# Regrouping the token tiles of the first mixture-of-experts pass, with a new hand-written plan of units

## The chip, the core and the metric

The kernel runs on one core of a Trainium2 chip. The metric is the device time of one execution in microseconds; each version's figure is the median of several runs. Engines are named as in the profile: PE is TensorE's matmuls, PEld its weight loads, DVE is VectorE, ACT ScalarE, POOL GpSimd, and SP the engine that issues most of the DMAs ("SPq", "POOLq" are queues).

## The reference

The input is `x`, 8 sequences of 512 tokens of 128 features, in 32-bit floats. A block of three parts is computed:

```python
x = x + 0.5 * ffn(layernorm(x))     # mixture of experts
x = x + attention(layernorm(x))     # 16 heads of 8, causal, partly rotary
x = x + 0.5 * ffn(layernorm(x))     # the same experts and weights again
```

In `ffn` a router (128 by 8) gives each token 8 logits. The two largest choose two experts, and their softmax gives two weights. An expert is `relu(x @ W1 + b1) @ W2 + b2`, 128 to 512 to 128 features; a token's result is the weighted sum of its two experts.

## The kernel before

**Tokens and passes.** A sequence is four tiles of 128 tokens. The feed-forward doesn't multiply every token with every expert. Tokens are normalised and routed by sequence, and each token's row is scattered twice, by indirect DMA from POOL, into a table in device memory (`xs`) that has room for `cap` rows per expert. Then the experts work through their rows. This is done in six passes, or groups: f0, f1, f2 for the first feed-forward, g0, g1, g2 for the second. Each group has its tiles of tokens and its room per expert (`ROOMS`: tiles, room, whether tagged). Before, f0 holds sequences 0 and 1 (8 tiles, room 351), f1 holds 2 to 4 and f2 holds 5 to 7 (12 tiles each, room 480); g0 holds 6 tiles (room 256), g1 and g2 hold 13 each (room 512). If an expert got more rows than its room, a flag would start a second, general path behind the main one.

**One expert of one group** (`experts`) is a list of pieces. SP fetches the expert's rows (`fetch`, L957; it waits for every scatter of the group). `turn` transposes the tiles on PE (L1000) and copies them out. Four `wide` pieces each multiply 128 of the 512 hidden features with all rows of the group's room (L1013) and apply bias and relu (L1020 on ACT, L1022 on DVE). One `out` piece per tile of rows multiplies back (L1037), adds the bias on DVE (L1041), and the last stores the expert's results by SP (L1048) into `ys`. A group of `ct` tiles of rows has 8 x (1 + 4 + `ct`) + 1 pieces: 65 for f0, 73 for f1, f2, g1 and g2, 57 for g0. `combine` then gathers each token's two results by indirect DMA (POOL) and adds them into `x`; in g1 and g2 POOL sends the results home instead (`send`, L981), and `collect` adds them.

**Routing** (`route`) is a stream of steps for one sequence: normalise in three steps (`layernorm`: statistics; aggregates on DVE and `rstd` on POOL; the scaling at L774 on DVE), transpose on PE (L789), logits (L825), ranks, places in the table (L869 and on), then the entry of eight scatters in a queue of jobs, then the gates. `project` does the same for attention's operands in eight steps: layernorm in three, transpose (L789), two for qkv (L1169), rotary, and the write of the operands' tiles.

**Attention** runs over 96 units, 12 to a sequence: 4 groups of 4 heads, 3 units each. A unit computes scores (L1231), their exp on ACT (L1238), a causal minimum with a mask on DVE (L1245), and the product with the values of the unit before (L1257). The score tile has one buffer.

**The order is written out by hand.** PE, ACT, DVE and SP execute in the order in which the program emits instructions, and the emission goes unit by unit, from -30 to 125 (0 to 95 hold attention). `plan` says for each group in which unit its first rows are fetched, and between which units its pieces are emitted. `surround(n)` emits unit n: scores, the values of the unit before, one piece of expert work, one transfer (a scatter or a gather from the queue of jobs), the streams that are `due` in this unit with some pieces between them, the rest of the unit's quota of pieces, and a second transfer where something urgent waits. `at(u, stream, steps, each)` puts `each` steps of a stream into each unit from u on. The quota is the rest of the group's pieces over the rest of its units, rounded up.

**What holds POOL back.** Every transfer waits for a "mark", the last relu, bias add or mask that was emitted before it (`behind_mark`), so that transfers don't bunch up ahead of the work. Before the first relu is emitted there is no mark. POOL's operations keep the program's order.

**Loading.** At the start SP loads the inputs and four experts' weights and clears the tables; the other weights, sequences and clears are issued two a unit from unit -30 on.

Of the kernel before, what the change touches and what calls it, by code (L numbers as in the profile page):

```python
# [21 lines left out]
B, N, D = 8, 512, 128  # L22
# [26 lines left out]
ROOMS = [(8, 351, False), (12, 480, False), (12, 480, False), (13, 512, True), (13, 512, True)]  # L49
# [1284 lines left out]
def macaron_kernel(  # L1334
# [51 lines left out]
    with ExitStack() as main:  # L1386
# [6 lines left out]
        f0 = m.open_group(whole(0, 1), 351, 0, "f0")  # L1393
        f1 = m.open_group(whole(2, 3, 4), 480, 1, "f1")
        f2 = m.open_group(whole(5, 6, 7), 480, 2, "f2")
# [40 lines left out]
        def routed(u, shares, urgent=False, ahead=False):  # L1436
# [6 lines left out]
            if shares[0][0] is not f1:  # L1443
                at(u, r, 3)
                u += 3
            at(u, r, steps)

        def combined(u, g, i, dst=None, urgent=False, ahead=False):
# [4 lines left out]
            (f0, first, first, -16), (f1, -17, -16, 7), (f2, 5, 7, 43), (g0, 41, 43, 79),  # L1453
            (g1, 78, 79, tail - 1), (g2, tail - 2, tail - 1, ends),
# [3 lines left out]
        def surround(n, att):  # L1458

            m.unit = n  # L1460
            now = None
            for g, fetch, start, end in plan:
# [5 lines left out]
                if start <= n < end:  # L1468
                    now, until = fills[g.key], end
                    if g is g1 and att:  # L1470
                        until = end + 7
            quota = min(now[1], -(-now[1] // (until - n))) if now else 0
# [30 lines left out]
            if n >= core and len(m.jobs) + len(m.results) > 2:  # L1503
# [8 lines left out]
        with m.banks(("m", 8)):  # L1512

            n = [m.normalise(b) for b in range(5)]
            r = [m.route([(f0, 0)], early=True), m.route([(f0, 1)], early=True),
                 m.route([(f1, 0)], True, early=True)]
# [3 lines left out]
            step(r[1], r[1], r[1], n[2], n[2])  # L1520
            transfers(8)
            step(n[3], n[3], n[4], n[4], *[r[0], r[1]] * 3, n[2], n[2])
            step(r[2], r[2], r[2], n[3], n[4], n[3], n[4])
            run(*r[:2], *n)
            m.bias_columns()

            at(first, r[2], 4)
            routed(first + 1, [(f1, 1)], urgent=True)
            routed(first + 3, [(f1, 2)], urgent=True)
            routed(-22, [(f2, 0)], urgent=True)  # L1530
            combined(-16, f0, 0, urgent=True, ahead=True)
            routed(-14, [(f2, 1)], urgent=True)
            combined(-12, f0, 1, urgent=True)
            routed(-10, [(f2, 2)], urgent=True)
            at(-10, m.project(0), 8)
            for b in range(B):
                u = b * seq
                if b == 2:
# [3 lines left out]
                if b > 0:  # L1542
                    at(u - 10, m.project(b), 8)
# [85 lines left out]
```

## Time and profile before

| | |
|---|---|
| median of 11 runs | 696.17 us (694.7 to 698.31) |
| profiled execution | 693.42 us, of which the span from first to last instruction is 691.7 |
| PE busy | 620.7 us, 90% of the span |
| DVE, ACT, POOL busy | 405.9, 342.9, 295.4 us |
| scores of unit 0 begin | 143.14 us |
| first transposes of g2 | 607.66 us |
| last matmuls of g2 begin | 665.72 us |

The profile is one execution. In a timeline a line gives the start, the duration of the (merged) instructions, engine, line of the kernel, operation, output and inputs, shape and count; in brackets stands how long the engine was idle before it and what released it. Matmuls are pipelined, so a single matmul's duration is longer than its distance to the next. In a row of slices each digit is the busy tenth of one fortieth of the span.

### The profile page before, as it was taken

The numbers are of one execution on the slowest core, as the hardware profiler recorded it, in microseconds if no ns is written. First come the engines' busy times: TensorE is split into PE (matmuls) and PEld (weight loads), VectorE is DVE, ScalarE is ACT, GpSimd is POOL, SyncE is SP. The second block draws the span as 40 slices with busy tenths as digits, with TensorE's granted clock in tenths as the row PEclk, the third lists the DMA queues.
The fourth block names the chain that finished last, engine by engine and source line by source line (L and its number), as shares of the span: only waits on it lengthen the run. The fifth ranks groups of instructions, "written<-read, shape, count | busy, mean of one in ns | idle before, by whom it ended". The sixth has DMA issues, their size and how long they took to land. (4 is left out here: it accounts for less than half of the span.)

```text
span 691.7 us, 12906 instructions
## 1 busy us (share of the span) xinstructions
PE 620.7 (90%) x4797; PEld 402.0 (58%) x4797; DVE 405.9 (59%) x1432; ACT 342.9 (50%) x552; POOL 295.4 (43%) x318
## 2 busy tenths in 40 slices
PE   3269999999999999999999999989999998989970
PEld 2148867766556556555656656555556566757760
DVE  6736438735466675675676687777666654333424
ACT  4034443454755665466466566566646542244420
POOL 3744637643122314325044324333244556665560
PEclk9999999999999999999999999999999999999995
DMA  8746843312409951001211101112202111154314
GB/s 266 197 136 196 223 115 100 85 49 78 100 20 159 209 169 38 27 24 46 68 32 44 52 26 37 31 32 77 56 28 63 32 58 39 47 152 137 90 55 153
DMA packets 80229, 61.32 MB, mean 89 GB/s; under 512 B 7400, under 2 KB 73888, under 8 KB 80160
## 3 DMA queue, kind: packets, MB, share of 16 engines
q1 hardware_dynamic: 71296, 42.79, 24.3%
q0 software_dynamic: 8576, 17.63, 8.5%
q8 instruction: 40, 0.66, 0.4%
q14 instruction: 29, 0.24, 0.1%
q10 hardware_dynamic: 288, 0.01, 0.0%
HBM read 26.21 MB, written 34.19 MB: 87 GB/s over the span
## 5 line engine op out<-in xcount | busy, mean ns | idle before, releaser
L1238 ACT ACTIVATE ee<-st 128x768 f32<-128x768 f32 (+1 forms) x192 | 159.0, 881 | 90.6 <-PE st L1231 86.7
L479 POOL DMA_INDIRECT yt_f<-ys,back_f x64 | 65.1, 1018 | 128.8 <-DVE ee L1245 55.9
L1245 DVE TENSOR_TENSOR ee<-ee,keep 128x256 f32<-128x256 f32 (+1 forms) x192 | 93.3, 507 | 22.1 <-ACT ee L1238 22.0
L1037 PEld LDWEIGHTS y_f<-w_sb,h_f 128*120 128x120 f32 (+1 forms) x704 | 85.9, 183 | 28.4 <-issue 16.2
L1231 PE MATMUL st<-qT,kT 32*128 32x512 f32 (+3 forms) x1024 | 96.1, 467 | 5.7 <-ACT kT L1214 3.3
L895 POOL DMA_INDIRECT xs<-xn_g,to_g x64 | 63.8, 997 | 84.5 <-DVE ee L1245 32.5
L1037 PEld LDWEIGHTS y_g<-w_sb,h_g 128*128 128x128 f32 x640 | 81.0, 192 | 32.2 <-issue 25.4
L1037 PE MATMUL y_f<-w_sb,h_f 128*120 128x128 f32 (+1 forms) x704 | 93.9, 277 | 0.2 <-DVE h_f L1022 0.2
L1013 PE MATMUL z_g<-xT_g,w_sb 128*128 128x512 f32 (+1 forms) x192 | 89.8, 554 | 1.3 <-DVE e_g L933 0.7
L1257 PE MATMUL o<-ee,vpad 128*32 128x512 f32 (+3 forms) x1024 | 89.6, 442 | 0.8 <-DVE ee L1245 0.8
L1013 PE MATMUL z_f<-xT_f,w_sb 128*128 128x480 f32 (+1 forms) x192 | 89.3, 554 | 1.0 <-ACT xT_f L1004 1.0
L1020 ACT ACTIVATE h_f<-z_f,b1T 128x480 f32<-128x480 f32 (+1 forms) x86 | 53.4, 622 | 68.7 <-PE z_f L1013 67.9
L1037 PE MATMUL y_g<-w_sb,h_g 128*128 128x128 f32 x640 | 85.6, 279 | 0.5 <-DVE o_tok L1280 0.3
L981 POOL DMA_INDIRECT ys<-ysb_g,home_g x64 | 62.8, 981 | 50.4 <-ACT h_g L1020 15.9
L1020 ACT ACTIVATE h_g<-z_g,b1T 128x512 f32<-128x512 f32 (+1 forms) x77 | 49.3, 642 | 54.3 <-PE z_g L1013 54.0
L1041 DVE TENSOR_TENSOR ysb_f<-y_f,b_sb 120x128 f32<-120x128 f32 (+1 forms) x88 | 25.1, 288 | 77.7 <-PE y_f L1037 74.0
L1041 DVE TENSOR_TENSOR ysb_g<-y_g,b_sb 128x128 f32<-128x128 f32 x80 | 23.1, 290 | 76.7 <-PE y_g L1037 72.8
L1231 PEld LDWEIGHTS st<-qT,kT 32*128 32x128 f32 x1024 | 43.1, 183 | 39.0 <-ACT kT L1214 11.4
L1257 PEld LDWEIGHTS o<-ee,vpad 128*32 128x32 f32 x1024 | 23.7, 108 | 52.4 <-issue 5.5
L895 POOL DMA_INDIRECT xs<-xn_n,to_f x40 | 39.0, 974 | 35.3 <-ACT xi_sb L732 8.4
L1013 PEld LDWEIGHTS z_g<-xT_g,w_sb 128*128 128x128 f32 x192 | 29.9, 194 | 21.2 <-issue 12.2
L1013 PEld LDWEIGHTS z_f<-xT_f,w_sb 128*128 128x128 f32 x192 | 30.5, 195 | 14.0 <-issue 7.4
(185 smaller groups left out, 768.3 us busy)
## 6 DMA issues: line engine op xcount, KB each, us to landing
xs<-zeros SPq DMA_DIRECT2D x8, 520.0 KB
xb_g<-xs SPq DMA_DIRECT2D x16, 260.0 KB
w_sb<-in_L_ffn_W_dram SPq DMA_DIRECT2D x16, 256.0 KB
xb_f<-xs SPq DMA_DIRECT2D x16, 240.0 KB
ys<-ysb_f SPq DMA_DIRECT2D x16, 240.0 KB
ys<-zeros SPq DMA_DIRECT2D x2, 1664.0 KB
x<-in_L_attn_x_dram SPq DMA_DIRECT2D x8, 256.0 KB
xs<-zeros SPq DMA_DIRECT2D x1, 1920.0 KB
```

The lines of the kernel that those rows point to most:

```text
L479: ins = op(*args, **kw)
L895: ins = nc.gpsimd.indirect_dma_start(out=g.xs[:, :], out_offset=bass.IndirectOffsetOnAxis(ap=to[:, t, r : r + 1], axis=0), in_=xn[:, t, : ...
L981: ins = nc.gpsimd.indirect_dma_start(out=g.ys[:, :], out_offset=bass.IndirectOffsetOnAxis(ap=home[e][:rows, t : t + 1], axis=0), in_=ys[:r ...
L1013: nc.tensor.matmul(z[:, :n], self.w1_sb[:, e, ts(c, P)], xT[:, n0 : n0 + n], start=True, stop=True,)
L1020: ins = nc.scalar.activation(dst, z[:, :n], AF.Relu, bias=bias)
L1037: nc.tensor.matmul(y[:rows], h[:, c, ts(t, rows)], self.w2_sb[:, e, c, :], start=(c == 0), stop=(c == C - 1),)
L1041: ins = nc.vector.tensor_tensor(ys[:rows, t, :], y[:rows], self.b2_sb[:rows, e], ALU.add)
L1231: nc.tensor.matmul(st[:, h, c0 : c0 + N - kt * P], kT[r0 : r0 + SLOT, ts(kt, P)], qT[r0 : r0 + SLOT, kt * P :], start=True, stop=True,)
L1238: nc.scalar.activation(ee[:, two, :width], st[:, two, :width], AF.Exp)
L1245: ins = self.nc.vector.tensor_tensor(d, d, self.keep.unsqueeze(1).unsqueeze(1).to_broadcast([P, 2, len(parts), P]), ALU.min,)
L1257: self.nc.tensor.matmul(self.o[h * SLOT : (h + 1) * SLOT, kt * P :], self.vpads[b % 2][:, kt, 4 * g + h, :], ee[:, h, c0 : c0 + n], start= ...
```

## The change

The first feed-forward takes the division that the second has: f0 gets sequence 0 and half of 1 (6 tiles, room 256), f1 the rest of 1, all of 2 and 3 and three tiles of 4 (13 tiles, room 512), f2 the last tile of 4 and 5 to 7 (13 tiles, room 512). So sequences 1 and 4 are routed into two groups at once, and combined from two. The pieces become 57 for f0 and stay at 73 for f1 and f2.

The plan moves with it: f0 takes 10 units instead of 14, f1 the units -20 to 0 instead of -16 to 6, f2 1 to 36 instead of 7 to 42, g0 38 to 73 instead of 43 to 78, and g1 starts at 74 instead of 79. Unit 37 has no expert work. In g0 and g1 the quota is spread evenly over attention's units instead of being rounded up in each. At the start f0's dispatch has 12 scatters instead of 16, the normalisations of sequences 2 to 4 are taken ahead of the last four of them, and units before -20 may take a third transfer. The projections of sequences 1 and 4 and their second routings take two steps a unit (`each`), the projections from 6 and 7 units ahead of the sequence's attention instead of 10.

```diff
-ROOMS = [(8, 351, False), (12, 480, False), (12, 480, False), (13, 512, True), (13, 512, True)]
+ROOMS = [(6, 256, False), (13, 512, False), (13, 512, False), (13, 512, True), (13, 512, True)]
...
-        f0 = m.open_group(whole(0, 1), 351, 0, "f0")
-        f1 = m.open_group(whole(2, 3, 4), 480, 1, "f1")
-        f2 = m.open_group(whole(5, 6, 7), 480, 2, "f2")
+        f0 = m.open_group([(0, 0, T), (1, 0, 2)], 256, 0, "f0")
+        f1 = m.open_group([(1, 2, T), *whole(2, 3), (4, 0, 3)], 512, 1, "f1")
+        f2 = m.open_group([(4, 3, T), *whole(5, 6, 7)], 512, 2, "f2")
...
-        def routed(u, shares, urgent=False, ahead=False):
+        def routed(u, shares, urgent=False, ahead=False, each=1):
             early = u < 0 or u > core
             r = m.route(shares, urgent, ahead, early)
             steps = 7 if early else 8
             if u > core:
                 at(u, r, 3 + steps, 3)
                 return
-            if shares[0][0] is not f1:
-                at(u, r, 3)
-                u += 3
-            at(u, r, steps)
+            at(u, r, 3 + steps, each)
...
         plan = [
-            (f0, first, first, -16), (f1, -17, -16, 7), (f2, 5, 7, 43), (g0, 41, 43, 79),
-            (g1, 78, 79, tail - 1), (g2, tail - 2, tail - 1, ends),
+            (f0, first, first, -20), (f1, -21, -20, 1), (f2, 0, 1, 37), (g0, 37, 38, 74),
+            (g1, 73, 74, tail - 1), (g2, tail - 2, tail - 1, ends),
         ]
...
                     now, until = fills[g.key], end
-                    if g is g1 and att:
-                        until = end + 7
-            quota = min(now[1], -(-now[1] // (until - n))) if now else 0
+                    quota = min(now[1], -(-now[1] // (until - n)))
+                    if g in (g0, g1) and att:
+                        until = end + 7 * (g is g1)
+                        quota = g.pieces - now[1]
+                        quota = g.pieces * (n + 1 - start) // (until - start) - quota
...
-            if n >= core and len(m.jobs) + len(m.results) > 2:
+            if (n >= core or n < -20) and len(m.jobs) + len(m.results) > 2:
                 run(take(fill, todo // 2))
                 todo -= todo // 2
                 m.transfer(second=True)
...
-            r = [m.route([(f0, 0)], early=True), m.route([(f0, 1)], early=True),
-                 m.route([(f1, 0)], True, early=True)]
+            r = [m.route(place[True][b], b > 1, early=True) for b in range(5)]
             step(n[0], n[0], n[1], n[1], n[0], n[0])
             step(r[0], n[1], n[1], r[0], r[1], r[0], r[0])
             transfers(8)
-            step(r[1], r[1], r[1], n[2], n[2])
-            transfers(8)
-            step(n[3], n[3], n[4], n[4], *[r[0], r[1]] * 3, n[2], n[2])
-            step(r[2], r[2], r[2], n[3], n[4], n[3], n[4])
-            run(*r[:2], *n)
+            step(r[1], r[1], r[1], n[2], n[2], n[3], n[3], n[4], n[4])
+            transfers(4)
+            step(*[r[0], r[1]] * 3)
+            run(*r[:2])
             m.bias_columns()
+            step(n[2], n[2], r[2], r[2], r[2], r[2])
 
             at(first, r[2], 4)
-            routed(first + 1, [(f1, 1)], urgent=True)
-            routed(first + 3, [(f1, 2)], urgent=True)
-            routed(-22, [(f2, 0)], urgent=True)
-            combined(-16, f0, 0, urgent=True, ahead=True)
-            routed(-14, [(f2, 1)], urgent=True)
-            combined(-12, f0, 1, urgent=True)
-            routed(-10, [(f2, 2)], urgent=True)
+            at(first, chain(n[3], r[3]), 10, 2)
+            at(first + 2, chain(n[4], r[4]), 10, 2)
+            routed(-21, place[True][5], urgent=True)
+            combined(-19, f0, 0, urgent=True, ahead=True)
+            routed(-16, place[True][6], urgent=True)
+            combined(-15, f0, 1, urgent=True)
+            routed(-12, place[True][7], urgent=True)
             at(-10, m.project(0), 8)
             for b in range(B):
                 u = b * seq
-                if b == 2:
-                    combined(7, f1, 0, urgent=True, ahead=True)
-                elif b > 2:
-                    combined(u - (17 if b == 5 else 21), *place[True][b][0], urgent=b == 5, ahead=b == 5)
-                if b > 0:
+                if b == 1:
+                    combined(1, f1, 0, urgent=True, ahead=True)
+                elif b == 4:
+                    combined(27, f1, 3)
+                    combined(37, f2, 0, urgent=True, ahead=True)
+                elif b > 1:
+                    combined(u - {2: 17, 7: 29}.get(b, 21), *place[True][b][0], urgent=b == 2, ahead=b == 2)
+                if b in (1, 4):
+                    at(u - 6 - (b == 4), m.project(b), 8, 2)
+                elif b > 0:
                     at(u - 10, m.project(b), 8)
                 for g in range(G):
                     at(u + g * per - 2, m.operands(b, g), 2)
                 at(u + seq + 2, m.finish(b), 2, 2 if b == B - 1 else 1)
-                routed(u + seq + (3 if b == B - 1 else 4), place[False][b], urgent=b in (1, 4, 5, 6, 7), ahead=b in (4, 6, 7))
+                routed(u + seq + (3 if b == B - 1 else 4), place[False][b], urgent=b in (1, 4, 5, 6, 7), ahead=b in (4, 6, 7), each=2 if b in (1, 4) else 1)
             for i in range(2):
-                combined(79 + 7 * i, g0, i, out)
+                combined(75 + 7 * i, g0, i, out)
```

More of the change, by code (lines that the diff above doesn't have):

```diff
@@ L1460, in surround @@
             m.unit = n
-            now = None
+            now, quota = None, 0
             for g, fetch, start, end in plan:
```

## The prediction, made before the changed kernel was run

> **What bounds the kernel now.** I read the page first, for the shares and the row of slices, then TensorE's own timeline for its idle places, then the timelines of the other engines around those places.
>
> ```profile
> PE 620.7 (90%) x4797; PEld 402.0 (58%) x4797; DVE 405.9 (59%) x1432; ACT 342.9 (50%) x552; POOL 295.4 (43%) x318
> PE   3269999999999999999999999989999998989970
> ```
>
> TensorE (PE) works 90% of the span, and nearly all of it between 40 and 671 us; it idles at the start, briefly before the last pass, and at the end. So a removed matmul is worth its own time, and any wait put into TensorE's stream costs its full length. A difference within 0.2% (1.4 us) I count as none, which is about what a measurement of this kernel can tell.
>
> ```profile
> 40.56 0.82 PE L1000 MATMUL xbT_ps_f<-ident,xb_f 117*128 117x117 f32 x3 [9.24 <-DMA xb_f<-xs]
> 72.98 0.47 PE L1000 MATMUL xbT_ps_f<-ident,xb_f 117*128 117x117 f32 x3
> 78.28 0.47 PE L1000 MATMUL xbT_ps_f<-ident,xb_f 117*128 117x117 f32 x3
> 91.76 0.60 PE L1000 MATMUL xbT_ps_f<-ident,xb_f 120*128 120x120 f32 x4 [0.84 <-DMA xb_f<-xs]
> 98.44 0.57 PE L1000 MATMUL xbT_ps_f<-ident,xb_f 120*128 120x120 f32 x4
> 105.58 0.57 PE L1000 MATMUL xbT_ps_f<-ident,xb_f 120*128 120x120 f32 x4
> 607.66 0.63 PE L1000 MATMUL xbT_ps_g<-ident,xb_g 128*128 128x128 f32 x4 [3.52 <-DMA xb_g<-xs]
> 624.14 0.60 PE L1000 MATMUL xbT_ps_g<-ident,xb_g 128*128 128x128 f32 x4
> 631.58 0.60 PE L1000 MATMUL xbT_ps_g<-ident,xb_g 128*128 128x128 f32 x4
> ```
>
> These are the first transposes of experts, on TensorE's timeline. Their distance prices one expert: 5.30 us at room 351 (f0), 7.14 at 480 (f1), 7.44 at 512 (g2). The bracketed ones start a pass, and wait for a fetch, which waits for the last scatter of that pass.
>
> ```profile
> 15.41 1.17 POOL L895 DMA_INDIRECT xs<-xn_n,to_f  x1 [7.65 <-DVE seen_f L915]
> 35.67 0.95 POOL L895 DMA_INDIRECT xs<-xn_n,to_f  x1 [0.30 <-issue]
> 47.11 1.03 POOL L895 DMA_INDIRECT xs<-xn_n,to_f  x1 [8.44 <-ACT xi_sb L732]
> 86.32 1.04 POOL L895 DMA_INDIRECT xs<-xn_n,to_f  x1 [0.30 <-DVE lg_f L829]
> 88.71 1.17 SPq L957 DMA_DIRECT2D xb_f<-xs  x2
> ```
>
> GpSimd (POOL) issues the scatters one by one, 1.27 us apart when nothing holds them. The first sixteen (15.41 to 35.67) set the start of f0. The next twenty-four are held until the third relu of expert 0 is done (47.11), and the last of them (86.32) is followed by f1's fetch 2.39 us later and by f1's first transpose 5.44 us later.
>
> **Part by part.** The profiled execution took 693.42 us around a span of 691.7; the median of the runs is 696.17. I add changes to 693.42, and then 2.75.
>
> *Start.* f0 needs 12 scatters instead of 16 (four fewer: 4 x 1.27 = 5.1), but the two rstd operations of sequences 3 and 4, which now follow the scatters at 36.64 (2.03 us together), go ahead of the last four. Gain 3.0: f0's first transpose at 37.6.
>
> *Expert work.* A tile of y costs 0.89 us at 128 rows, four transposes 0.43, a z of 512 columns 0.865 (g2's rows). One of 256 columns I take in proportion, 0.433; the highest row for it is 0.54, between attention's operations. f0's expert becomes 0.22 + 4 x 0.433 + 2 x 0.89 = 3.73, eight are 29.9 instead of 42.4. f1 and f2 grow from 7.14 to 7.44, sixteen times: +4.9.
>
> *Wait for f1's dispatch, moved and new.* From 40.56 to 90.92 f0's stretch holds 42.4 of experts, 4.3 of three routings and 3.6 of slow start. After, it is 29.9 + 2 x 1.35 + 3.6 = 36.2, as sequence 5's transposes and logits (1.2) fall into f1's stretch. So TensorE is free at 73.8. But f1 now takes 26 scatters. One is free to go at once; the next stands behind the same third relu, which comes about 5.7 us after f0's first transpose (6.55 before, with wider z's): 43.3. From there 25 scatters and 1.25 us of constants on the same queue: the last one starts at 43.3 + 24 x 1.27 + 1.25 = 75.0, and f1 at 75.0 + 5.44 = 80.4. The wait is then 6.6 us instead of 0.84. Bounds: none, if the marks do not hold POOL (the scatters would end near 68); 9, if some more do. I take the row's own pace, 6.6, so f1 starts 11.4 earlier than at 91.76, and the 1.2 comes back behind it. SP's loads are also queued in this stretch, but the experts' weights are issued some 10 us before use, and a delay there is covered by the wait for dispatch.
>
> *A cold TensorE.* By stretches (busy time of each engine, then TensorE's granted clock, DMA share, GB/s):
>
> ```profile
> 88.00:92.00 4.00, 3.15 (x29) 2.97 (x29) 2.19 (x8) 0.55 (x1) 0.00 (x0) 1.00 0.61 176
> 608.00:612.00 4.00, 3.33 (x10) 1.86 (x9) 2.56 (x9) 1.46 (x3) 3.09 (x4) 0.64 0.90 269
> ```
>
> After 0.84 us of idle time the granted clock stayed at 1.00; after the 3.52 before 607.66 it was 0.64, the first z took 1.96 us instead of 1.02, and up to 615.49 TensorE needed 7.83 us for 5.2 of work and 0.67 of waiting: 2.0 lost. f1 now starts after a longer idle time, so +2.0. [...]
>
> *Doubled steps.* `project` of sequences 1 and 4 and the second routing of the same two take two steps a unit. Step 3 normalises (DVE, L774), step 4 transposes the result on TensorE (L789). Before, they lay a unit apart:
>
> ```profile
> 271.39 0.93 PE L1231 MATMUL st<-qT,kT 32*128 32x384 f32 x8
> 277.15 1.11 DVE L774 TENSOR_SCALAR xn_a<-x,mv_a,rstd_a 128x128 f32<-128x128 f32 x4
> 278.58 0.60 PE L789 MATMUL xnT_ps_a<-ident,xn_a 128*128 128x128 f32 x4
> 284.46 1.11 DVE L774 TENSOR_SCALAR xn_g<-x,mv_g,rstd_g 128x128 f32<-128x128 f32 x4
> 285.21 0.93 PE L1231 MATMUL st<-qT,kT 32*128 32x384 f32 x8
> 288.41 0.60 PE L789 MATMUL xnT_ps_g<-ident,xn_g 128*128 128x128 f32 x4
> ```
>
> The unit begun at 271.39 ended when the next scores started, at 275.59, but its normalise ran at 277.15: VectorE works off exp's mask, the evacuations and the copies first, and runs some 2 us behind TensorE. Had the transposes stood in that unit, TensorE would have waited for them until 278.3, with the unit's last piece of expert work and all later scores queued behind. I work out the four units: in 7 the normalise would end 6.5 us after the scores begin, the transposes 0.3 later, the last piece 0.9 later, 7.7 against 4.65 + 0.43: 2.6. In 42 two normalises come together (sequence 2's routing is there too): 2.1. In 29 and 65 VectorE still carries project's normalise from the unit before: 2.9 each. Sum 10.5; I take 9.5, since VectorE catches up in the wait. Lower bound 4 x 1.1 = 4.4, from the unit that began at 280.19 and was long enough (5.02) for its normalise to end only 0.36 after it; upper 13. The other doubled pairs lie on VectorE or ScalarE alone, and I cost them at nothing, covered by TensorE's 4 to 5 us a unit; without that cover they are about 1 us.
>
> *The rest of the plan.* f2's fetch has one unit before its first piece: +0.7 (0 to 4: 2.4 + 3.05 us after the last scatter, against a unit of 3.4 and 1.9 of scores and values). Unit 37 has no expert work: +0.5 (the one-piece units at 447 and 450 waited 0.6 to 0.7). Attention's 96 units take 173 pieces instead of 188; a switch between shapes costs about 0.09 there, so -1.3. g0 has fifteen one-piece units either way, spread instead of at the end; the waits there were 3.4 in all, and I let them stand. The tail gives three pieces to attention: same work, and the chain from the last attention to g2 shortens by what TensorE did earlier. Together 0.
>
> **Sum.** -11.4 (f1's start) + 1.2 + 4.9 + 2.0 + 9.5 + 0 = +6.2: 699.6 for the profiled execution, 702.4 for a median. The tokens of the busiest expert in the three passes, counted from the given inputs, are 206, 474 and 486, under 256, 512 and 512, so the general path stays off.
>
> **Rivals.**
> - *The doubled steps are hidden* (faster). One mechanism: VectorE, with fewer expert pieces in these units, reaches the normalise as TensorE reaches the transposes. It decides from 3.3 us for all four downward, where the sum turns negative; at 1 us in all it gives 693.9. For it: the transposes at 288.41 came long after their normalise. Against: 277.15, well after its own unit. Chance 0.17.
> - *The dispatch keeps up*: POOL isn't held, f1 starts 0.84 after TensorE is free, warm. 5.8 and 2.0 fall away: 694.6. Against: 47.11, and a pace of 1.27 that leaves 33 us of issuing in a stretch of 36. Chance 0.13.
> - *f2's dispatch is late as well*: 36 issues of POOL in twenty units, the last in the unit before the fetch; 4 us of wait and 2 of cold clock: 708. Chance 0.15.
>
> **How the numbers follow.** The forecast has 0.55. Faster by over 0.2%: 0.14 of the first rival, 0.08 of the second, 0.03 of the forecast's low end: 0.25. Within: 0.03 + 0.05 + 0.02 = 0.10. Slower: 0.65. For the range, the low end takes the first rival nearly whole and the second (692.5); the high end takes the third and pairs at their upper bound with half its price (709.0). About 2 in 10 are left outside. The likeliest case's own range is 698 to 707.
>
> **What would show it.** Right: f0's first transpose near 37.6; experts 3.7 apart; TensorE idle 5 to 8 us before f1 with "DMA xb_f<-xs" as its releaser, and slow z's after it; four waits of TensorE at L789 on DVE's `xn_a` and `xn_g` in attention, 2 to 3 us each. Wrong: no such waits, or an f1 that starts by 76. An attention stretch shorter by over 5 us would mean that I mispriced the pairs.

## The result, and the profile after

The change made the kernel slower: 719.24 us against 696.04 for the kernel before beside it, a ratio of 1.033 (95%: 1.0313 to 1.0347). The prediction was 702.4 with a range up to 709, so the direction was right and the size was not. The profiled spans are 717.0 and 691.7 us: 25.3 to account for, where the prediction had 6.2.

From the page of the kernel after, the busy times and the row of slices:

```profile
PE 624.0 (87%) x4727; PEld 402.3 (56%) x4727; DVE 411.0 (57%) x1440; ACT 336.7 (47%) x542; POOL 297.7 (42%) x318
PE   3289499999899999899898989889999997979970
```

TensorE is busy 3.3 us more than before and idle 22.0 more (93.0 against 71.0). The 4 in the fifth slice is new. On TensorE's own timeline it is f1's wait, and the four waits that the prediction named stand in attention:

```profile
37.37 0.66 PE L1000 MATMUL xbT_ps_f<-ident,xb_f 128*128 128x128 f32 x2 [3.22 <-DMA xb_f<-xs]
86.16 1.09 PE L1000 MATMUL xbT_ps_f<-ident,xb_f 128*128 128x128 f32 x4 [9.68 <-DMA xb_f<-xs]
190.11 1.10 PE L789 MATMUL xnT_ps_a<-ident,xn_a 128*128 128x128 f32 x4 [1.99 <-DVE xn_a L774]
293.91 1.01 PE L789 MATMUL xnT_ps_g<-ident,xn_g 128*128 128x128 f32 x4 [1.93 <-DVE xn_g L774]
353.12 1.10 PE L789 MATMUL xnT_ps_a<-ident,xn_a 128*128 128x128 f32 x4 [2.68 <-DVE xn_a L774]
452.15 1.20 PE L789 MATMUL xnT_ps_g<-ident,xn_g 128*128 128x128 f32 x4 [2.71 <-DVE xn_g L774]
```

f0 starts 3.2 us earlier than before, f1 only 5.6 (86.16 against 91.76; predicted 80.4). The whole of attention in one stretch, first of the kernel before, then of the kernel after (stretch, length, busy time of PE, PEld, DVE, ACT, POOL, then TensorE's clock, DMA share, GB/s):

```profile
143.14:562.20 419.06, 411.72 (x3531) 243.25 (x3531) 270.68 (x863) 250.34 (x397) 145.89 (x143) 1.00 0.26 62
```

```profile
156.38:586.00 429.62, 408.04 (x3451) 237.03 (x3450) 275.55 (x868) 242.52 (x380) 144.89 (x140) 0.99 0.24 60
```

Attention is 10.6 us longer although 80 matmuls have left it: idle time grew from 7.3 to 21.6, and busy time fell by 3.7 where the groups of expert work (L1000, L1013, L1037) fell by 11.1. By stages, after less before:

| stage | after − before |
|---|---|
| start to f0's first transposes | −3.2 |
| f0 and the wait, to f1's first transposes | −2.4 |
| f1's start to unit 0's scores | +18.8 |
| attention | +10.6 |
| attention's end to g2 | +0.5 |
| g2 to the end | +1.0 |
| sum | +25.3 |

The 18.8 is mostly work that moved there: 70 of f1's 73 pieces instead of 52 lie ahead of attention. So two places are left to explain: why f1's start gained so little, and why attention grew while it lost work.

Every ratio is against the kernel before, run beside it on the same chip. The kernel before took 695 to 697 us beside e1 to e13 and 707 to 708 beside e14 to e19. Chip 5 of the record is in both groups (696.20 beside e5 to e8, 707.40 beside e18 and e19), so whether the chip or the time of the measurement makes this difference is open. Stretches and waits come from one profiled execution of each kernel.

### The profile page after: what moved, and what is told of

Read it like the earlier page. It is cut to its first block, busy times and chain, and to the rows that moved or that the text cites. A ratio compares the mean times of both kernels' runs of the same rounds, so it can differ in the third digit from the quotient of the medians.

```text
span 717.0 us, 12758 instructions
## 1 busy us (share of the span) xinstructions
PE 624.0 (87%) x4727; PEld 402.3 (56%) x4727; DVE 411.0 (57%) x1440; ACT 336.7 (47%) x542; POOL 297.7 (42%) x318
## 5 line engine op out<-in xcount | busy, mean ns | idle before, releaser
L1231 PE MATMUL st<-qT,kT 32*128 32x512 f32 (+3 forms) x1024 | 97.0, 471 | 10.3 <-ACT kT L1214 8.4
L1037 PEld LDWEIGHTS y_g<-w_sb,h_g 128*128 128x128 f32 x640 | 81.5, 193 | 33.2 <-issue 27.0
L1037 PEld LDWEIGHTS y_f<-w_sb,h_f 128*128 128x128 f32 x640 | 80.7, 191 | 26.2 <-issue 17.7
L1013 PE MATMUL z_g<-xT_g,w_sb 128*128 128x512 f32 (+1 forms) x192 | 91.2, 560 | 0.7 <-ACT xT_g L1004 0.7
L1013 PE MATMUL z_f<-xT_f,w_sb 128*128 128x512 f32 (+1 forms) x192 | 88.0, 552 | 1.5 <-ACT xT_f L1004 1.1
L1037 PE MATMUL y_g<-w_sb,h_g 128*128 128x128 f32 x640 | 86.6, 280 | 0.8 <-ACT h_g L1020 0.8
L1037 PE MATMUL y_f<-w_sb,h_f 128*128 128x128 f32 x640 | 86.9, 279 | 0.3 <-DVE h_f L1022 0.3
L1020 ACT ACTIVATE h_f<-z_f,b1T 128x512 f32<-128x512 f32 (+1 forms) x83 | 50.1, 606 | 60.3 <-PE z_f L1013 60.2
L1020 ACT ACTIVATE h_g<-z_g,b1T 128x512 f32<-128x512 f32 (+1 forms) x68 | 43.8, 644 | 51.9 <-PE z_g L1013 51.7
L1041 DVE TENSOR_TENSOR ysb_f<-y_f,b_sb 128x128 f32<-128x128 f32 x80 | 23.0, 289 | 73.8 <-PE y_f L1037 73.6
L1013 PEld LDWEIGHTS z_g<-xT_g,w_sb 128*128 128x128 f32 x192 | 30.3, 197 | 24.2 <-issue 16.4
L1013 PEld LDWEIGHTS z_f<-xT_f,w_sb 128*128 128x128 f32 x192 | 31.8, 200 | 14.9 <-issue 5.9
```

The source lines that it names most:

```text
L1013: nc.tensor.matmul(z[:, :n], self.w1_sb[:, e, ts(c, P)], xT[:, n0 : n0 + n], start=True, stop=True,)
L1020: ins = nc.scalar.activation(dst, z[:, :n], AF.Relu, bias=bias)
L1037: nc.tensor.matmul(y[:rows], h[:, c, ts(t, rows)], self.w2_sb[:, e, c, :], start=(c == 0), stop=(c == C - 1),)
L1041: ins = nc.vector.tensor_tensor(ys[:rows, t, :], y[:rows], self.b2_sb[:rows, e], ALU.add)
L1231: nc.tensor.matmul(st[:, h, c0 : c0 + N - kt * P], kT[r0 : r0 + SLOT, ts(kt, P)], qT[r0 : r0 + SLOT, kt * P :], start=True, stop=True,)
```

## The experiments

Theory A: the doubled steps cost attention its time. Theory B: the expert work that left attention took its cover with it, and the chain of exp sets the units' pace. Theory C: SP's and POOL's queues, not TensorE, set f1's start.

### What a piece of expert work is worth in attention

**e8_before_f1_early** changes one number of the kernel before, so that units 1 to 6 have no expert work.

```diff
-            (f0, first, first, -16), (f1, -17, -16, 7), (f2, 5, 7, 43), (g0, 41, 43, 79),
+            (f0, first, first, -16), (f1, -17, -16, 1), (f2, 5, 7, 43), (g0, 41, 43, 79),
```

> The kernel before with the second pass of the first feed-forward ended before unit 1 instead of unit 7; units 1 to 6 then have no expert work and its 18 pieces lie ahead of attention. The same work is done. The prediction's credit (a piece that leaves attention takes its TensorE time with it, wherever it goes): within 1.5 us of the kernel before, 694 to 697. Theory B (a unit does not go below some 3.2 us of scores, exp and the next scores, since there is one buffer for the scores): seven units fall from 33.9 to 23 or so while the stretch before grows by 17, and the time is 5 to 8 us longer, 700 to 703, with ACT ee or kT as releaser of the scores' waits.

696.09 us, ratio 1.0013 (0.9995 to 1.003): no difference. Its stretches from f1's start to unit 0 and from there to attention's end:

```profile
91.80:155.00 63.20, 61.99 (x386) 46.71 (x387) 35.85 (x149) 28.53 (x52) 32.20 (x33) 1.00 0.32 83
155.00:562.20 407.20, 397.47 (x3441) 232.16 (x3441) 267.71 (x852) 246.32 (x391) 146.21 (x143) 1.00 0.26 63
```

From f1's first transposes on, the first grew from 51.4 us (91.76 to 143.14) to 63.0 (91.99 to 155.0); attention shrank from 419.1 to 407.2. Units without expert work took 2.6 to 3.3 us, most of them less than the 3.2 that theory B takes as a floor, and units 0 to 6 together 22.0 instead of 33.9. A piece takes its time with it. For these units theory B is out, and the prediction's credit for moved work was right; later units were not tested in this way.

**e4_quota_rounded** puts the old, rounded-up quota back into the kernel after; **e9_before_even** puts the new even one into the kernel before.

```diff
-                    if g in (g0, g1) and att:
-                        until = end + 7 * (g is g1)
-                        quota = g.pieces - now[1]
-                        quota = g.pieces * (n + 1 - start) // (until - start) - quota
+                    if g is g1 and att:
+                        until = end + 7
```

> The changed kernel with the quota of g0 and g1 rounded up in each unit, as before the change, instead of spread evenly. Theory B in a milder form (the even spread leaves more units of attention with one piece): 2 to 5 us off. Theory A: within 2 us of the changed kernel, 717 to 721.

> The kernel before with one part of the change alone: the pieces of the second feed-forward's first two passes spread evenly over their units instead of rounded up. In the changed kernel the even spread was worth 2.7 us (e4_quota_rounded). If it is worth the same here: 692 to 694. If it only mattered there because of what lay under the doubled steps: 695 to 697.

e4: 721.91 us, 1.0377 (1.0335 to 1.0419), outside both expectations. Against the kernel after (1.033) the even spread is worth some 3 us, though the intervals just overlap; a mild theory B would have it the other way. e9: 1.0009 (0.9988 to 1.003), nothing. It would fit both that the even spread helps only where doubled steps have made units uneven, but no run shows it.

### The price of the doubled steps

**e7_before_doubled** adds the doubled steps to the kernel before, and enters sequence 7's gathers eight units earlier, as the change does. **e3_before_doubled**, the same without moving the gathers, gave no time.

```diff
-                    combined(u - (17 if b == 5 else 21), *place[True][b][0], ...
+                    combined(u - {5: 17, 7: 29}.get(b, 21), *place[True][b][0], ...
-                if b > 0:
+                if b in (1, 4):
+                    at(u - 6 - (b == 4), m.project(b), 8, 2)
+                elif b > 0:
                     at(u - 10, m.project(b), 8)
...
-                routed(..., ahead=b in (4, 6, 7))
+                routed(..., ahead=b in (4, 6, 7), each=2 if b in (1, 4) else 1)
```

> The kernel before with the doubled steps alone: project and the second routing of sequences 1 and 4 at two steps a unit, at the changed kernel's units (and sequence 7's gathers entered eight units earlier, which that needs). Theory A (the prediction's term: a normalise and its transposes in one unit hold TensorE whatever else is there): four waits at L789 of 2 to 3 us and 695 + 8 to 12 = 703 to 707. Theory B (the attention of the changed kernel lost its time because 15 pieces of expert work no longer cover it): in the fuller units of the kernel before the pairs cost under 4 us: 695 to 699.

714.84 us, ratio 1.0282 (1.0243 to 1.0321): 18.6 us, above both theories, and four fifths of what the whole change lost. Its four runs lie between 710.76 and 717.95, and the profile is of the fastest. Its attention:

```profile
143.20:578.40 435.20, 415.11 (x3531) 244.57 (x3531) 271.85 (x863) 250.49 (x397) 146.16 (x143) 1.00 0.24 60
```

16.1 us more than before, with the same matmuls: 12.8 idle and 3.4 busy. The idle part is four waits at L789 (1.98, 2.66, 2.42, 3.22: 10.3, where the prediction had added up 10.5), and 1.9 more for `kT`, most of it in one place. TensorE's timeline at the last pair, unit 65, and three units on:

```profile
444.52 1.02 PE L789 MATMUL xnT_ps_g<-ident,xn_g 128*128 128x128 f32 x4 [3.22 <-DVE xn_g L774]
...
463.33 1.14 PE L1231 MATMUL st<-qT,kT 32*128 32x512 f32 x8 [2.21 <-ACT kT L1214]
```

`kT` is a copy on ScalarE. ScalarE's timeline there says why it was late:

```profile
462.58 0.23 ACT L929 ACTIVATE ex_g<-ex_g 128x32 f32<-128x32 f32 x1 [2.18 <-DVE ex_g L925]
462.71 0.57 ACT L1214 COPY kT<-kT_ps 128x512 f32<-128x512 f32 x1
```

The routing's steps 9 and 10 are a subtraction on VectorE (L925) and its exp on ScalarE (L929). Doubled, they share a unit. VectorE, behind with the masks, subtracts at 462.35; ScalarE waits 2.18 us for that with an instruction of 0.23, the copy of `kT` stands behind it, and TensorE's next scores stand behind the copy. In the kernel after the same pair costs 1.34 us (315.07) and 1.14 (471.44). Of the busy 3.4, 1.7 is half clock after the wait of 3.22 (granted clock 0.50 from 446 to 448); 1.7 I can't assign.

**e10_before_doubled_apart** and **e1_steps_apart** lay the dependent steps a unit apart, with as many units as in the doubled form: e10 on e7, with the exp's pair; e1 on the kernel after, without it.

```diff
-                due.setdefault(u + k // each, []).append((stream, 1))
+                v = k // each
+                if each == 2 and steps in (8, 11):
+                    v = (0, 0, 0, 1, 2, 2, 3, 3, 3, 4, 5)[k]                # e10
+                    v = 0 if k < 3 else max(k // 2, 1)                      # e1
+                due.setdefault(u + v, []).append((stream, 1))
```

> The changed kernel, but the doubled streams take 3, 1, 2, 2 (and so on) steps in successive units instead of 2, 2, 2, 2: normalising and transposing lie a unit apart again, and every later step stays where it was. Theory A (the same-unit pairs cost the time): the four waits of TensorE for xn_a and xn_g (1.99, 1.93, 2.68 and 2.71 us) and the two slow-clock stretches after the longer ones go: 11 to 15 us off, about 705 to 708. Theory B (attention is uncovered, since it has 173 pieces of expert work instead of 188, and the exp chain sets the pace of a unit): the waits only change their name, under 4 us off, 715 or more.

> e7_before_doubled, with the dependent steps a unit apart although two still run in most units: normalise and transposes, and the routing's subtraction on VectorE and its exp on ScalarE, no longer share a unit. Theory A (the 18 us of e7_before_doubled are the two kinds of dependent pair, 10.3 of waits for xn and 2.2 for kT, and the half clock after them): 698 to 703. Rival E (the cost is that the same steps stand in half as many units, whatever their order: later units have no use for what is taken from them): 708 to 714.

e1: 714.46 us, 1.0287 (1.0254 to 1.0319), with a span 5.8 us shorter than the kernel after: near theory B's 715 and far from theory A's 705 to 708. e10: 711.44 us, 1.0206 (1.017 to 1.0242) against e7's 1.0282, in rival E's range and not in theory A's. So the order of the steps is worth 3 to 5 us, and the dependent pairs are the smaller part of the price. Some 15 us of e7's loss remain in e10's time. Its attention, in the same terms as above:

```profile
146.30:577.90 431.60, 417.61 (x3531) 245.32 (x3531) 271.13 (x863) 250.38 (x397) 145.75 (x143) 0.99 0.25 61
```

That is 12.5 us more than before, 6.7 idle and 5.9 busy. Another 3.2 lie ahead of unit 0 (146.30 against 143.14), where the edit changes nothing, so not all of what e10's time lost is the doubled steps. In e10 the exp's pair is gone (`kT` back to 3.3 us), but with three steps of layernorm in one unit VectorE itself now waits 1.22 us for POOL's `rstd`, and TensorE waits in smaller portions (0.53, 0.99, 0.72, 1.32, 0.76 at L789, and 1.14 for `qT`) with two spells of half clock behind them (0.50 from 288 to 290 and from 448 to 450). The waits are still for VectorE: by these rows it is the engine that has no room for twice the steps in those units, though no run took work off it.

### What holds f1's start

The scatters of the kernel after on POOL's timeline (the first held one, and the last of f1), then SP's queue:

```profile
43.48 0.96 POOL L895 DMA_INDIRECT xs<-xn_n,to_f  x1 [8.73 <-ACT h_f L1020]
...
77.07 0.96 POOL L895 DMA_INDIRECT xs<-xn_n,to_f  x1 [0.30 <-DVE mv_f L766]
```

```profile
73.73 0.37 SPq L1048 DMA_DIRECT2D ys<-ysb_f  x1
80.59 0.52 SPq L705 DMA_DIRECT2D xs<-zeros  x1
81.23 1.82 SPq L957 DMA_DIRECT2D xb_f<-xs  x2
```

POOL's first held scatter starts where it was predicted (43.3), its last 2.1 us later than predicted (75.0). But f1's fetch (81.23) stands behind a clear of the third pass's table (80.59), and that clear behind the first scatter into the same table: tile 3 of sequence 4, which the change sends to f2 and POOL issues right after f1's last. The waits of SP's queue give it 6.4 us.

**e2_clears_first** issues the four clears earlier; **e5_clears_first_no_marks** also takes the marks away from the scatters of this stretch; **e12_constants_late** also issues attention's constants (copies on POOL among them) at unit −18.

```diff
         self.loads.insert(6, partial(self.load_x, 6))
+        self.loads.extend(partial(self.clear, 2, t) for t in range(4))          # e2, e5, e12
         self.loads.extend([
...
-        if self.mark is not None:
+        if self.mark is not None and self.unit > -21:                           # e5, e12
...
-                if u == first:
+                if u == -18:                                                    # e12
                     m.attention_constants()
```

> The changed kernel, with the four clears of f2's table ahead of the last weights and sequence in the list of loads. Theory C (the last clear, issued behind the first scatter into the table that it clears, waited 6.4 us for it and held f1's fetch on SP's queue behind it): the fetch is issued at 79.5 instead of 81.2, and lands in 3 instead of 4.9 us, so f1 starts at about 82.6 instead of 86.2; 3 to 4 us off, about 715.5. Rival (the scatters of f1 alone set its start): under 1 us.

> The changed kernel with the four clears of the third pass's table issued early (as in e2_clears_first) and with no marks before unit -21, so that GpSimd's scatters for the second pass are not held behind ScalarE's relus. Theory C (f1's start is set by queues: SP's clear took 3.3 of it, the held scatters the rest): the wait of TensorE before f1 falls from 9.7 (6 to 7 in e2_clears_first) to under 2 us, f1 starts warm near 78, and the time is 5 to 7 us below e2_clears_first: 709 to 711. Rival D (the marks keep the scatters out of the way of the weights' loads, DMA share 0.71 in f0's stretch): TensorE then waits inside f0 for w_sb or xb_f instead, and the time is within 2 us of e2_clears_first: 714 to 718.

> e5_clears_first_no_marks with attention's constants issued at unit -18 instead of unit -30. There, with the marks gone, GpSimd still stood 6.5 us at the constants' first copy (43.88), which waits for VectorE's decay, and then issued scatters without a pause. Theory C' (GpSimd's stop, by marks or by constants, sets f1's start): the scatters for the second pass begin near 38, f1's wait falls from 5.4 to 0 or 1, its clock stays full, and the time is 5 to 7 us below e5_clears_first_no_marks: 708 to 710. Rival: the routing of sequences 2 to 4 comes no earlier than now (their transposes stand in TensorE's order behind f0's first), so the scatters have nothing to issue, and the gain is under 2: 713 to 715.

e2: 715.95 us, 1.0307 (1.0283 to 1.0331); f1 starts at 82.24 instead of 86.16, and the span is 4.8 shorter. The interval overlaps that of the kernel after, so it is the trace that shows this gain. e5: 715.17, 1.0273 (1.0256 to 1.029), 0.8 us below e2 by the time and 2.4 by the ratio: in rival D's range, but not for its reason. POOL's timeline in e5:

```profile
43.88 0.72 POOL L479 COPY qpad<-decay 128x16 f32<-128x16 f32 x4 [6.51 <-ACT ex_f L929]
```

With the marks gone, POOL stands at the next thing in its queue, attention's constants, until the same time. e12 takes these away too. POOL then issues f1's last scatter at 66.51, ten microseconds earlier, and yet f1 starts at 80.09 and the time is 714.09 (1.0258, 1.0229 to 1.0287). By stretches of e12:

```profile
66.00:70.00 4.00, 4.00 (x30) 3.72 (x29) 0.69 (x3) 2.03 (x5) 1.17 (x2) 1.00 1.00 272
70.00:74.00 4.00, 4.00 (x28) 3.63 (x27) 1.50 (x8) 1.68 (x4) 0.00 (x0) 1.00 1.03 278
```

The DMA share (last but one) is 1.00 to 1.03 while the third pass's clears, f0's stores and the loads are under way. From SP's queue, a store of f0 and f1's fetch behind it:

```profile
73.54 0.60 SPq L1048 DMA_DIRECT2D ys<-ysb_f  x1
...
74.78 1.24 SPq L957 DMA_DIRECT2D xb_f<-xs  x2
```

The fetch goes out 8.3 us after the last scatter (2.4 in the kernel before), and f1 starts 5.3 us behind it (3.05 before). The rival's number came true, but its reason didn't: POOL had scatters to issue. One queue after the other let go, and what was left is the fetch's place in SP's queue and a slower transfer.

### Parts together, and the early start without the doubled steps

**e6_apart_clears_no_marks** joins e1 and e5; **e11_all** joins e12 and e10's order of steps.

> e1_steps_apart, the early clears and no marks together, on the changed kernel. If the causes are independent, the gains add: 719.2 - 4.8 (steps apart) - 3.3 (clears) - 5 to 7 (marks, by theory C) = 704 to 706; by rival D (marks give nothing) 711 to 713.

> e12_constants_late with the dependent steps laid apart as in e10_before_doubled. Gains added: e12's 708 to 710 less some 5 to 7 for the steps (e6 showed 5 without the exp's pair, whose two waits for kT in the changed kernel are 1.34 and 1.14): 702 to 704.

e6: 710.13 us, 1.0207 (1.0169 to 1.0246), between the two expectations and nearer rival D's. e11: 705.81, 1.0148 (1.0119 to 1.0176), 2 us above its own. More than half of the loss is given back; the waits for `kT` at 315 and 471 are gone as expected. What remains lies in attention, by comparison with e13 below: from unit 0's scores to the last values it takes 423.5 us against 409.9, with only three pieces more.

**e13_seven_tiles_no_pairs** keeps the early start, with e12's edits, and drops what forced the doubling: f0 takes 7 tiles (its busiest expert has 233 tokens, counted from the given inputs, under the room of 256), f1 13 and f2 12 at room 480, and attention's plan is that of the kernel before, except that f2 starts in unit 1 and the even spread stays. Of the doubled streams only sequence 1's projection remains, with its normalise and transposes a unit apart.

```diff
-ROOMS = [(6, 256, False), (13, 512, False), (13, 512, False), ...
+ROOMS = [(7, 256, False), (13, 480, False), (12, 480, False), ...
...
-        f1 = m.open_group([(1, 2, T), *whole(2, 3), (4, 0, 3)], 512, 1, "f1")
-        f2 = m.open_group([(4, 3, T), *whole(5, 6, 7)], 512, 2, "f2")
+        f1 = m.open_group([(1, 3, T), *whole(2, 3, 4)], 480, 1, "f1")
+        f2 = m.open_group(whole(5, 6, 7), 480, 2, "f2")
...
-            (f0, first, first, -20), (f1, -21, -20, 1), (f2, 0, 1, 37), (g0, 37, 38, 74),
+            (f0, first, first, -20), (f1, -21, -20, 1), (f2, 0, 1, 43), (g0, 41, 43, 79),
```

> The early start of the change without the steps that it doubles in attention: passes of 7, 13 and 12 tiles at rooms 256, 480 and 480, so that only one tile of sequence 1 lies in the second pass and no tile of sequence 4 in the third; the plan of attention's units as in the kernel before (third pass to unit 43, then 43 to 79), every second routing at one step a unit, and of the doubled projects only sequence 1's, its normalise and transposes a unit apart; the early clears, no marks and late constants of e12_constants_late kept. Theory A with C (the start gains, the doubled steps in attention lose): f1 starts at 78 to 80 instead of 91.8 (-12 to -13), sequence 5's transposes and logits come behind it (+1.2), a cold start of f1 (+1.7), one project doubled (+1 to 2): 695.7 - 8 = 686 to 690. Rival F (attention without its 18 pieces of f1, and a third pass that starts six units sooner, give part of the gain back whatever the steps): 692 to 698.

694.66 us, ratio 0.9974 (0.9959 to 0.999): 0.3% faster than the kernel before beside it, in rival F's range and far from theory A's 686 to 690. Attention is 9.9 us shorter than before, but f1 starts later than the 78 to 80 expected:

```profile
153.50:562.70 409.20, 396.68 (x3426) 230.92 (x3426) 271.46 (x861) 243.91 (x383) 141.28 (x138) 1.00 0.26 61
```

```profile
84.86 1.03 PE L1000 MATMUL xbT_ps_f<-ident,xb_f 120*128 120x120 f32 x4 [6.92 <-DMA xb_f<-xs]
```

(In e8, also with 18 pieces fewer, attention was 11.9 us shorter.) POOL's last scatter for f1 starts at 70.97 and SP issues the fetch at 79.32, so 5 to 6 of the expected 12 to 13 us at f1's start are missing. The cold start, put at 1.7, was 3.2: 6.5 us of f1's work up to 92 ran at a granted clock of 0.50.

**e14_early_fetch** (f1 closed and fetched at unit −23, two more transfers a unit before it) and **e17_loads_after_fetch** (the clears, `wqkv`, sequence 7 and `wo` behind that fetch) are edits of e13; **e15_all_early_fetch** and **e16_after_early_fetch** put e14's edit into e11 and into the kernel after.

```diff
-            (f0, first, first, -20), (f1, -21, -20, 1), ...                       # e14, e15, e16
+            (f0, first, first, -20), (f1, -23, -20, 1), ...
...
             run(take(fill, todo))
+            for _ in range(2 if n < -23 else 0):
+                m.transfer(second=True)
...
-                for _ in range(min(2, len(m.loads))):                              # e17
+                for _ in range(min(2, max(len(m.loads) - (7 if u < -20 else 0), 0))):
```

> e13_seven_tiles_no_pairs with f1 closed and its first fetch issued at unit -23 instead of -21 (and two more transfers a unit before it, so that all scatters are out by then). Theory G (the fetch stands on SP's queue behind f0's last stores): it is issued right after the last scatter has landed, near 73.5, f1 starts at 77 to 79 instead of 84.9 with 0 to 1 us of wait and a full clock, and the time is 6 to 8 us below e13: 687 to 689. Rival H (the transfers are late, or SP's waiting fetch holds f0's stores and weights, so that TensorE waits inside f0): 692 to 696.

> e11_all with the same earlier fetch of f1. By theory G its wait of 3.9 us before f1 and the half clock behind it fall away: 705.8 - 4 to 6 = 700 to 702. By rival H: 704 to 707.

> The changed kernel with the same earlier fetch and nothing else. Marks and constants still hold GpSimd, and the last scatter of f1 still goes out near 75 to 77; but the fetch no longer stands behind the last clear of the third pass's table, whose 6.4 us of waiting held it. Theory C (with G): as much as the early clears gave or a little more, 719.2 - 3 to 5 = 714 to 716. Rival H: 718 to 721.

> e13_seven_tiles_no_pairs with seven transfers that nothing needs before unit -12 (four clears of the third pass's table, wqkv, x of sequence 7, wo) held until f1's first fetch is out. Theory J (the DMA engines are full from 60 us on, share 0.9 to 1.0, and f1's scatters and fetch share them with these seven): the share there falls to 0.7, f1's fetch is issued by 75 instead of 79.3 and lands sooner, its wait falls from 6.9 to 1 to 4 us, and the ratio to the kernel before from 0.9974 to 0.988 to 0.993 (687 to 691 on a chip where the kernel before takes 696). Rival K (f1's start is held by f0's own stores and scatters, whatever lies among them): ratio 0.996 to 0.999.

Ratios: e14 1.0019 (0.9994 to 1.0045), e15 1.0277 (1.0238 to 1.0316), e16 1.0315 (1.0273 to 1.0356), e17 1.0081 (1.0055 to 1.0107). By themselves they say little on their theories, because f0 in them takes 15 to 19 us longer from its first expert's transposes to its eighth's than in the kernels that they start from, with waits inside f0 that those didn't have. The base had to be run beside an edit: **e18_seven_tiles_again** is e13 unchanged, and **e19_fetch_and_loads** is e13 with both edits, on one chip.

> e13_seven_tiles_no_pairs once more, unchanged, as the base for the run beside it. If its gain holds on another chip: ratio 0.995 to 0.999. If f0's stretch, with more transfers in less time, suffers more on a chip where the kernel before takes 707 us: ratio 1.000 to 1.010 there, and stops in f0 as in e14 and e17.

> e13_seven_tiles_no_pairs with both edits: f1 closed and first fetched at unit -23, and the seven transfers that nothing needs yet held behind that. If the order of the transfers holds f1's start (theories G and J), f1 starts at 77 to 80 instead of 84.9 where f0 isn't stopped, and the ratio is 0.007 to 0.010 below that of e18. If not (H and K), within 0.003 of e18's or above it.

e18: 710.61 us, 1.0026 (0.9998 to 1.0055); e19: 707.02, 0.9991 (0.9967 to 1.0015). TensorE in e18, in the middle of f0, at its eighth expert and at f1's start, then the eighth expert and f1's start in e19:

```profile
72.21 0.21 PE L869 MATMUL pos_ps_f<-mask_f,earlier 128*128 128x32 bf16 x1 [4.51 <-DVE mask_f L848]
...
87.52 0.38 PE L1000 MATMUL xbT_ps_f<-ident,xb_f 128*128 128x128 f32 x2
...
98.13 1.03 PE L1000 MATMUL xbT_ps_f<-ident,xb_f 120*128 120x120 f32 x4 [2.72 <-DVE xn_f L774]
```

```profile
85.25 0.63 PE L1000 MATMUL xbT_ps_f<-ident,xb_f 128*128 128x128 f32 x2
...
93.91 0.57 PE L1000 MATMUL xbT_ps_f<-ident,xb_f 120*128 120x120 f32 x4
```

The kernel of e13 has the long f0 here as well, so the edits don't cause it: ScalarE stands 5.37 us in it up to 70.44 with "remote" as releaser, and from 70 to 74 the DMA share is 0.14. With both edits f1 starts 4.2 us earlier and with no wait, and its first transposes take 0.57 us instead of 1.03. (The profile names VectorE for e18's wait of 2.72, but the transposes read `xb_f`, whose fetch SP had not issued by 90.) Of the 4.2, 2.3 had been gained by f0's eighth expert; the other 1.9 are f1's start itself. The medians differ by 3.6 us, but the ratios by 0.0035, which is 2.5 us, and their intervals overlap. So the traces show that the place of the fetch and the loads around it held f1's start, and a gain in time is not clear of noise. Which of the two matters more wasn't separated on one chip; on others, e14 (the fetch alone) starts f1 at 94.45 without a wait and e17 (the loads alone) at 98.45 after 1.28 us, which points to the fetch. e19 was not run beside a kernel before of 696 us, and no version was shown to be faster than the kernel before in both groups of measurements.

## Why the prediction was right in direction and wrong in size

**Start: right.** 37.37 against 37.6. The steady distance of f0's experts is 3.73 us, as worked out from 256 columns (61.12 to 64.85 to 68.59).

**Wait for f1's dispatch: the step that failed first, 5.8 us.** The pace of the scatters was nearly right (77.07 against 75.0). What failed is the last link, "f1 at 75.0 + 5.44": from the last scatter to f1 it took 9.1 us, of which 4.2 up to the fetch (2.39 before) and 4.9 behind it (3.05 before). With it failed the sentence that SP's loads are covered. They are covered for the weights; but the change also sends a scatter into the third pass's table before f1's fetch, and the clear of that table, which SP holds ahead of the fetch, has to wait for it. The queue that a moved step passes was named and not followed in order. e2 gives back 3.9 us at f1's start by that one reordering. The rival "the dispatch keeps up" fell with it: freed of POOL's stops (e12), f1 still waits 4.05 us for DMAs. f0's own stretch was also put 2.9 us too short (39.1, from 37.37 to 76.48, against 36.2); that cost nothing, since the fetch came later still.

**A cold TensorE: right** for f1 (2.17 us of work at clock 0.50 up to 89 and 4.00 at 0.75 up to 93: 2.1 lost, 2.0 predicted), and left out in attention, where the waits of 2.68 and 2.71 us cost 3.4 more:

```profile
354.00:356.00 2.00, 2.00 (x13) 0.72 (x16) 1.30 (x3) 0.13 (x1) 0.00 (x0) 0.50 0.00 0
```

**Doubled steps: the waits were right, the price was not.** The four waits sum to 9.31 us; 9.5 was the term. But e7 prices the same edit at 16.1 us of attention. The missing 6.6 are 0.8 of longer waits than the term (10.3), the clause "the other doubled pairs lie on VectorE or ScalarE alone, and I cost them at nothing" (1.9: a pair across the two engines stops ScalarE's queue, and with it `kT`), the half clock behind a long wait (1.7 in e7), 0.6 of other waits and 1.7 of busy time without a cause. The upper bound of 13 didn't hold either: it bounded the sum of the waits at one place and not what stands behind them. Nor is the mechanism more than a part of it: with normalise and transposes a unit apart (e10) the term's own waits shrink, and attention still loses 12.5 us. What is left goes with the density of the steps, or with the later place of the projections (6 and 7 units ahead instead of 10), which no run parts; the prediction had a term for neither. The rival "the doubled steps are hidden" is ruled out, in a kernel with more cover (e7) as in this one.

**Expert work moved out of attention: right.** e8 shows it at full value for the 18 pieces of units 1 to 6, and theory B, which I formed after the result, fell on it for those units.

**The rest of the plan, put at 0.** From attention's end on nothing was gained, though the three pieces given to attention (2.1 us of expert work) had left: the stages there are 1.5 longer. g2's stretch (85.0 us after, 84.0 before) takes 83.5 to 85.6 in e7 to e10, which have g2's plan of before, so the 1.0 there is not shown to be the change's. The shortening that I set against the pieces didn't come. f2's dispatch, the third rival, was not late. Of the waits that the prediction let stand, those for `kT` grew: they are 3.3 us in attention before, 4.9 with the even spread alone (e9), 6.2 in e11 and 7.0 in e13, where the exp's pair is gone.

**The account of 19.1 us** between 6.2 and 25.3: 5.8 for f1's start; 6.6 for the doubled steps as e7 prices them, and 1.7 for a second spell of half clock in attention; 1.5 behind attention. About 3.5 is not assigned to a cause; the waits for `kT` (8.4 us, 3.2 more than in e7) would cover most of it, but no run prices them by themselves.

## What to carry to other kernels

Price steps that are packed closer by a run that packs them alone (e7), and not only by the dependent pairs that this creates: with the pairs apart, 12.5 of attention's 16.1 us stayed. Look for such pairs across all engines, and ask of each waiting instruction what is queued behind it: a 0.23 us exp that waits holds the copy that the next scores need. When a pass is split so that one source feeds two tables, walk each queue in emission order: a clear ahead of a fetch now waits for a scatter that was never on its path. And test what looks like lost cover by moving work alone: the kernel before, with 18 pieces moved out of attention (e8), paid nothing for it.

## What was unexpected in the hardware

- The granted clock didn't follow the length of a wait. Behind a wait of 1.98 us at the first doubled normalise it was 0.50 in e12 (186 to 188 us) and 1.00 in e7 (182 to 184). In e5 a wait of 1.93 us was followed by half clock, in e7 a wait of 2.66 us was not. The wait, then the stretch behind it, first of e5, then of e7:

```profile
290.15 1.02 PE L789 MATMUL xnT_ps_g<-ident,xn_g 128*128 128x128 f32 x4 [1.93 <-DVE xn_g L774]
```

```profile
292.00:294.00 2.00, 2.00 (x7) 1.02 (x5) 0.69 (x1) 0.58 (x1) 0.00 (x0) 0.50 0.00 0
```

```profile
283.19 1.01 PE L789 MATMUL xnT_ps_g<-ident,xn_g 128*128 128x128 f32 x4 [2.66 <-DVE xn_g L774]
```

```profile
284.00:286.00 2.00, 2.00 (x18) 1.77 (x17) 1.38 (x2) 0.58 (x1) 0.00 (x0) 1.00 0.12 33
```

  What sets the clock behind a wait, if not its length, these runs don't show.
- The same kernel (e13, e18) took 694.66 and 710.61 us in two measurements, on chips 7 and 5, with most of the difference in f0's stretch, where ScalarE stood 5.37 us with "remote" as releaser and the DMA share fell to 0.14. What it waited for the runs don't show.
- Sixteen DMA engines reached a share of 1.0 at 272 to 278 GB/s in e12, with clears, stores, loads and scatters mixed.
